# Cross-attention scores from one folded matrix per head, four heads in one matmul

## The chip, the cores and the metric

The kernel runs on one NeuronCore of a Trainium2 chip. Its time is the device time of one execution in microseconds. Times of a kernel are given as the median of several runs; a profiled execution has a time of its own, and its trace a span from the first to the last instruction.

## The reference, cut to what matters

The network has four blocks on 16 sequences of 128 tokens with 128 features; everything is f32. The change is in the second attention of the first block:

```python
def mha(xq, ctx, wq, wk, wv, wo, bo):              # H = 16 heads, DH = 64
    q = (xq @ wq).reshape(b, sq, H, DH).transpose(0, 2, 1, 3)
    k = (ctx @ wk).reshape(b, sk, H, DH).transpose(0, 2, 1, 3)
    v = (ctx @ wv).reshape(b, sk, H, DH).transpose(0, 2, 1, 3)
    scores = jnp.einsum('bhqd,bhkd->bhqk', q, k) / math.sqrt(DH)
    attn = jax.nn.softmax(scores, axis=-1)
    out = jnp.einsum('bhqk,bhkd->bhqd', attn, v)
    return out.transpose(0, 2, 1, 3).reshape(b, sq, INNER) @ wo + bo

h1 = adaln(x, t, norm1_w, norm1_b)
x = mha(h1, h1, ...attn1...) + x                   # self: 128 keys a sequence
h2 = adaln(x, t, norm2_w, norm2_b)
x = mha(h2, context, ...attn2...) + x              # cross: 77 keys a sequence
```

Since each score is h2 Wq_h (ctx Wk_h)^T for head h, it can also be computed as h2 (Wq_h Wk_h^T) ctx^T, with a 128 x 128 matrix per head. A gated feed-forward, a mixture of experts, slot attention and a second mixture of experts follow.

## The kernel before, in words

Attention works in 16 groups (`NG`), each of two sequences (`GB`): groups 0 to 7 are the self-attention of all 16 sequences, groups 8 to 15 the cross-attention. Here they are called the self half and the cross half. A unit is one sequence of one group; 32 units run one after the other.

`attn_prologue` (L235) makes what a group needs. It normalizes the tokens (za, on VectorE), transposes them (ta, L224) and applies scale and shift on ScalarE into hT (tile `ha`, L251), features on partitions. Then it projects on TensorE: queries with eight 128-column weight blocks against 256 tokens, keys with eight blocks against 256 (self) or 154 (cross) tokens, two blocks to a PSUM tile `pq` (L267), each tile read out by one ScalarE copy (L268); and values `pv` (L272, L276). A 128-column block holds two heads, on partitions 0 to 63 and 64 to 127 of `q` and `k`.

`scores` (L279) is called twice for a unit, for eight heads each (`hg`, here a head half). Eight matmuls with 64 contraction rows, alternating between the two halves of the partitions, write a PSUM tile `s` of two banks (L286). Softmax follows: VectorE's maximum (L294) and subtraction (L296), ScalarE's exp (L297), VectorE's sum and reciprocal (L299, L300), GpSimd's multiplication (L301). `attend_t` (L304) transposes the weights (te, L311), with one copy on ScalarE and one on VectorE (L312); `attend_v` (L315) multiplies by the values (po, L321), with a copy of the first head half on ScalarE and of the second on VectorE (L325); `attn_project` (L327) applies wo (ya, L331) and adds to `r`.

The loop at L379 runs one unit behind: the prologue of the next group is issued with the first unit of a group, the scores of the next unit come ahead of the transposes of this one, and the output projection is that of the unit before. The source order is not the final one: a scheduler places the instructions of each engine when the program is built, so pieces of scores lie between projections and po matmuls in the trace.

Pools that matter: PSUM `psS` (tag s, two tiles of two banks), `psT` (transposes, two), `psM` (tag mm, two: projections, values, po, ya); SBUF `zp` (tags z and h, two each), `att` (tags q, k, v, two each). The weights of both attentions are loaded at the start, four tiles of 128 x 2048 (`w_att`, L115, L121); `_layout` (L1061) arranges them on the host, wq beside wk for each attention.

Of the kernel before, what the change touches and what calls it, by code (L numbers as in the profile page):

```python
# [10 lines left out]
F32 = mybir.dt.float32  # L11
# [7 lines left out]
P = 128  # L19
B = 16  # L20
D = 128
NC = 77
H = 16
DH = 64
# [32 lines left out]
def pixart_kernel(  # L57
# [174 lines left out]
    GB = 2  # L232
    GT = GB * P

    def attn_prologue(g, ap_):  # L235
        ph, gi = divmod(g, B // GB)
        b0 = gi * GB
        rg = r[:, b0 : b0 + GB, :]
        z = zp.tile([P, 4, D], F32, name=f"za{g}", tag="z")
        if ph == 0:  # L240
            xg = x0[:, b0 : b0 + GB, :]
            rs, mean = ln_stats(xg, P, GB, f"i{g}")
            normalize(rg, xg, rs, mean, GB)
        rs, mean = ln_stats(rg, P, GB, f"j{g}")
        normalize(z, rg, rs, mean, GB)
        row_add(rg, R_BO1 if ph == 0 else R_BO2, GB)
        t = transpose_n(z, P, GB, f"a{g}")
        hT = zp.tile([P, 512], F32, name=f"ha{g}", tag="h")
        for i in range(GB):
            b = b0 + i  # L250
            S.activation(  # L251
                hT[:, i * P : (i + 1) * P], t[:, i, :], AF.Identity,
                bias=ada_sh[:, ph, b : b + 1], scale=ada_sc[:, ph, b : b + 1],
            )
        hT = hT[:, :GT]
        nk = P if ph == 0 else NC
        kvT = hT if ph == 0 else ctxT[:, b0 * NC : (b0 + GB) * NC]
        wqk, wvo = w_att[2 * ph], w_att[2 * ph + 1]
        qT = ap_.tile([P, 8, GT], F32, name=f"q{g}", tag="q")
        kT = ap_.tile([P, 8, GT], F32, name=f"k{g}", tag="k")  # L260
        v = ap_.tile([P, GB, H, DH], F32, name=f"v{g}", tag="v")
        for dst, src, w0, n in ((qT, hT, 0, GT), (kT, kvT, 1024, GB * nk)):
            for c in range(0, 8, 2):
                pq = psM.tile([P, 2, 256], F32, name=f"pq{g}_{w0}_{c}", tag="mm")
                for j in range(2):
                    w = w0 + (c + j) * P
                    PE.matmul(pq[:, j, :n], lhsT=wqk[:, w : w + P], rhs=src, start=True, stop=True)  # L267
                S.copy(dst[:, c : c + 2, :n], pq[:, :, :n])  # L268
        for i in range(GB):
            for hh in range(2):  # L270
                pv = psM.tile([P, 8, DH], F32, name=f"pv{g}_{i}_{hh}", tag="mm")
                PE.matmul(  # L272
                    pv[:nk].rearrange("p h d -> p (h d)"), lhsT=kvT[:, i * nk : (i + 1) * nk],
                    rhs=wvo[:, hh * 512 : (hh + 1) * 512], start=True, stop=True,
                )
                S.copy(v[:nk, i, hh * 8 : (hh + 1) * 8, :], pv[:nk])  # L276
        return dict(ph=ph, b0=b0, nk=nk, qT=qT, kT=kT, v=v, wo=wvo, g=g)

    def scores(st, i, hg, ap_):  # L279

        nk, nm = st["nk"], f"{st['g']}_{i}_{hg}"
        ps = psS.tile([P, 2, 512], F32, name=f"s{nm}", tag="s")
        for j in range(4):
            for par in range(2):
                h0, c = par * DH, 4 * hg + j
                PE.matmul(  # L286
                    ps[:, par, j * nk : (j + 1) * nk],
                    lhsT=st["qT"][h0 : h0 + DH, c, i * P : (i + 1) * P],
                    rhs=st["kT"][h0 : h0 + DH, c, i * nk : (i + 1) * nk],
                    start=True, stop=True,  # L290
                )
# [12 lines left out]
    def attend_t(st, i, hg, e, ap_):  # L304

        nk, nm = st["nk"], f"{st['g']}_{i}_{hg}"
        eT = ap_.tile([P, 2, 4, P], F32, name=f"eT{nm}", tag="eT", bufs=3)
        for par in range(2):
            t = psT.tile([P, 4, P], F32, name=f"te{nm}_{par}", tag="t")
            for j in range(4):  # L310
                PE.transpose(t[:nk, j, :], e[:, par, j, :], ident)  # L311
            (S.copy if par == 0 else V.tensor_copy)(eT[:nk, par], t[:nk])  # L312
        return eT
# [59 lines left out]
    if True:  # L373
        units = [(g, i) for g in range(NG) for i in range(GB)]
        states = {0: attn_prologue(0, ap_)}
        e_next = [scores(states[0], 0, hg, ap_) for hg in range(2)]
        late = None
        glu_h = {}
        for n, (g, i) in enumerate(units):  # L379
            if i == 0:  # L380
                if g + 1 < NG:
                    states[g + 1] = attn_prologue(g + 1, ap_)
                else:
                    glu_h[0] = glu_prologue(0)
            e = e_next
            if n + 1 < len(units):
                g1, i1 = units[n + 1]
                e_next = [scores(states[g1], i1, hg, ap_) for hg in range(2)]
            oT = ap_.tile([P, 8, P], F32, name=f"oT{g}_{i}", tag="oT")
            eT = [attend_t(states[g], i, hg, e[hg], ap_) for hg in range(2)]  # L390
            if late:
                attn_project(*late)
            for hg in range(2):
                attend_v(states[g], i, hg, eT[hg], oT)
            late = (states[g], i, oT)
        attn_project(*late)

# [663 lines left out]
def _layout(a):  # L1061
    import numpy as np

    cat = np.concatenate

    def chunks(w):
        return cat(np.split(w, w.shape[0] // P, axis=0), axis=1)

    def column(*vs):
        return cat([v.reshape(-1, P).T for v in vs], axis=1)  # L1070

    l0, l1 = "L0_xcond_", "L1_xcond_"
    cols = column(
        *[a[f"{l0}norm{k}_b"] for k in (1, 2, 3)], a[l0 + "ff_b1"],
        *[a[l1 + n] for n in ("lnkv_g", "lnkv_b", "lnq_g", "lnq_b", "lnm_g", "lnm_b", "bk", "bv", "bq", "b1")],
    )
    rows = cat(
        [a[l0 + n].ravel() for n in ("attn1_bo", "attn2_bo", "ff_b2")]
        + [a[l1 + n].ravel() for n in ("q_mu", "q_logsig", "lnp_g", "lnp_b", "bu", "b2")]
        + [a["cond_1024"].ravel(), a["L0_ffn_rb"], a["L1_ffn_b_gate"], np.arange(8, 0, -1, dtype=np.float32)]  # L1080
    )[None]
    attn = []
    for k in ("attn1_", "attn2_"):
        attn.append(cat([a[l0 + k + "wq"], a[l0 + k + "wk"]], axis=1))
        attn.append(cat([a[l0 + k + "wv"], chunks(a[l0 + k + "wo"])], axis=1))
    f = "L0_ffn_"
    gs = [a[f + "sg"], *a[f + "rg"]]
    us = [a[f + "su"], *a[f + "ru"]]
    ds = [a[f + "sd"], *a[f + "rd"]]

    def wide(w):
        return cat([w, np.zeros((w.shape[0], IP - I0), np.float32)], axis=1)

    moe0 = [cat([wide(g.T), wide(u.T), chunks(wide(d).T)], axis=1) for g, u, d in zip(gs, us, ds)]

    moe1 = [
        cat([w1, chunks(w2), b1.reshape(-1, P).T, np.broadcast_to(b2, (P, D))], axis=1)
        for w1, w2, b1, b2 in zip(*[a["L1_ffn_" + n] for n in ("W1", "W2", "b1", "b2")])
    ]
# [36 lines left out]
```

## Time and profile before

| | |
|---|---|
| median of 3 runs | 962.75 us (961.74 to 963.99) |
| profiled execution | 961.27 us, span 959.5 us |
| mean granted TensorE clock | 0.939 |
| attention ends at about | 488 us of the span |
| PE L267 (projections) | 97.3 us with 256 columns, 22.7 us with 154 columns busy |
| PE L286 (scores) | 45.5 us in the self half, 41.5 us in the cross half busy |
| ACT L268 copies | 584 ns (128 x 512), 412 ns (128 x 308) each |

PE is TensorE's matmuls, PEld its weight loads, DVE VectorE, ACT ScalarE, POOL GpSimd. Busy time on PE counts modelled ends that overlap the next start, so lengths are best read from start to start. In the group lines, "64*128" stands for the contraction rows and output columns of the array in use, "out<-in" for tiles by name. The chain is the work that ended last, followed back from the end.

### The profile page before, as it was taken

The numbers are of one execution on the slowest core, as the hardware profiler recorded it, in microseconds if no ns is written. First come the engines' busy times: TensorE is split into PE (matmuls) and PEld (weight loads), VectorE is DVE, ScalarE is ACT, GpSimd is POOL, SyncE is SP. The second block draws the span as 40 slices with busy tenths as digits, with TensorE's granted clock in tenths as the row PEclk, the third lists the DMA queues.
The fourth block names the chain that finished last, engine by engine and source line by source line (L and its number), as shares of the span: only waits on it lengthen the run. The fifth ranks groups of instructions, "written<-read, shape, count | busy, mean of one in ns | idle before, by whom it ended". The sixth has DMA issues, their size and how long they took to land.

```text
span 959.5 us, 16967 instructions
## 1 busy us (share of the span) xinstructions
PE 830.1 (87%) x6155; PEld 660.3 (69%) x6155; DVE 646.5 (67%) x1946; ACT 416.5 (43%) x873; POOL 369.9 (39%) x416
## 2 busy tenths in 40 slices
PE   5799999999999999999999978999746677775597
PEld 4477767677687777777866647999645556654586
DVE  4896668766775654555867794555687776768454
ACT  2445554455444444554342211444135767552132
POOL 2442323222322211233252206776254544443476
PEclk9899999999999999999999988999859998976699
DMA  8100000000000000000020015998300000012794
GB/s 325 40 2 1 1 1 2 1 1 1 1 2 1 1 1 2 1 1 1 2 71 12 23 61 166 320 331 271 99 1 1 1 1 1 1 31 58 253 341 149
DMA packets 29422, 61.87 MB, mean 64 GB/s; under 512 B 4250, under 2 KB 17901, under 8 KB 28699
## 3 DMA queue, kind: packets, MB, share of 16 engines
q1 hardware_dynamic: 25067, 51.70, 15.9%
q0 software_dynamic: 4272, 9.09, 3.1%
q8 instruction: 49, 0.80, 0.3%
q14 instruction: 34, 0.28, 0.1%
HBM read 54.01 MB, written 7.23 MB: 64 GB/s over the span
## 4 chain that ended last, share of the span: by engine, by line
PE 56%; DVE 21%; POOL 8%; DMA 7%; ACT 4%; issue 4%; SPq 0%; POOLq 0%; ACTq 0%; DVEq 0%
PE pq L267 11%; PE s L286 6%; PE po L321 5%; PE pv L272 5%; PE te L311 5%; PE ya L331 4%; DMA res<-ysm,tom 3%; PE gum L735 2%; PE h1n L979 2%; ACT eT L312 2%; DMA zsm<-tok,frmm 2%; PE su L898 2%; DMA zsn<-tok,frmn 2%; PE ynn L994 1%; POOL ym L170 1%
## 5 line engine op out<-in xcount | busy, mean ns | idle before, releaser
L301 POOL TENSOR_TENSOR e<-e,ri 128x1024 f32<-128x1024 f32 (+1 forms) x64 | 99.9, 1562 | 297.5 <-DVE ri L300 129.1
L294 DVE TENSOR_REDUCE mx<-s 128x8 f32<-128x1024 f32 (+1 forms) x64 | 64.3, 1006 | 95.7 <-PE s L286 95.7
L267 PE MATMUL pq<-ha,wa 128*128 128x256 f32 x384 | 97.3, 406 | 0.9 <-ACT ha L251 0.9
L286 PEld LDWEIGHTS s<-k,q 64*128 64x128 f32 x1024 | 69.9, 187 | 40.6 <-issue 40.5
L286 PE MATMUL s<-k,q 64*128 64x128 f32 (+1 forms) x1024 | 87.0, 287 | 8.1 <-DVE e L296 8.1
L311 PE MATMUL te<-ident,e 128*128 128x128 f32 (+1 forms) x512 | 75.7, 280 | 12.9 <-ACT eT L312 12.0
L267 PEld LDWEIGHTS pq<-ha,wa 128*128 128x128 f32 x384 | 70.6, 198 | 19.0 <-ACT q L268 3.6
L299 DVE TENSOR_REDUCE ri<-e 128x8 f32<-128x1024 f32 (+1 forms) x64 | 64.0, 1001 | 21.0 <-ACT e L297 20.8
L331 PE MATMUL ya<-wa,oT 128*128 128x128 f32 x512 | 72.4, 275 | 0.0
L311 PEld LDWEIGHTS te<-ident,e 128*128 128x128 f32 (+1 forms) x512 | 55.6, 144 | 23.7 <-ACT eT L312 8.5
L312 ACT COPY eT<-te 128x512 f32<-128x512 f32 (+1 forms) x64 | 37.3, 582 | 79.6 <-PE te L311 79.5
L321 PE MATMUL po<-eT,v 128*64 128x128 f32 (+1 forms) x1024 | 69.9, 278 | 0.0
L297 ACT ACTIVATE e<-e 128x1024 f32<-128x1024 f32 (+1 forms) x64 | 56.9, 891 | 29.5 <-DVE e L296 28.6
L296 DVE TENSOR_TENSOR e<-s,mx 128x1024 f32<-128x1024 f32 (+1 forms) x64 | 64.3, 1007 | 3.9 <-DVE mx L294 0.5
L331 PEld LDWEIGHTS ya<-wa,oT 128*128 128x128 f32 x512 | 64.4, 192 | 0.4 <-ACT oT L325 0.4
L321 PEld LDWEIGHTS po<-eT,v 128*64 128x64 f32 (+1 forms) x1024 | 56.4, 136 | 7.2 <-ACT oT L325 0.8
L735 PE MATMUL gum<-zTnm,wm 128*128 128x128 f32 x456 | 61.3, 275 | 0.0
L735 PEld LDWEIGHTS gum<-zTnm,wm 128*128 128x128 f32 x456 | 56.8, 192 | 0.3 <-ACT zTnm L650 0.2
L268 ACT COPY q<-pq 128x512 f32<-128x512 f32 x64 | 37.3, 584 | 45.3 <-PE pq L267 45.3
L636 POOL DMA_INDIRECT zsm<-tok,frmm x38 | 36.9, 970 | 34.1 <-DVE secm L614 21.1
L276 ACT COPY v<-pv 128x512 f32<-128x512 f32 (+1 forms) x64 | 37.4, 584 | 21.8 <-PE pv L272 21.1
L312 DVE COPY eT<-te 128x512 f32<-128x512 f32 (+1 forms) x64 | 42.7, 669 | 5.3 <-PE te L311 5.3
(368 smaller groups left out, 1805.6 us busy)
## 6 DMA issues: line engine op xcount, KB each, us to landing
wm<-in_moe_w_dram SPq DMA_DIRECT2D x38, 576.0 KB, 5.1
wn<-in_moe_w_dram SPq DMA_DIRECT2D x23, 578.0 KB, 5.5
wa<-in_attn_w_dram SPq DMA_DIRECT2D x4, 1024.0 KB, 7.5
ygm<-res SPq DMA_DIRECT2D x8, 256.0 KB, 3.8
tok<-stm SPq DMA_DIRECT2D x4, 258.0 KB, 3.3
tok<-stn SPq DMA_DIRECT2D x4, 258.0 KB, 3.2
x<-in_x_dram SPq DMA_DIRECT2D x8, 128.0 KB, 7.1
cb<-in_rows_dram SPq DMA_DIRECT2D x1, 1024.0 KB, 8.7
```

What stands on the lines that cost most here:

```text
L267: PE.matmul(pq[:, j, :n], lhsT=wqk[:, w : w + P], rhs=src, start=True, stop=True)
L286: PE.matmul(ps[:, par, j * nk : (j + 1) * nk], lhsT=st["qT"][h0 : h0 + DH, c, i * P : (i + 1) * P], rhs=st["kT"][h0 : h0 + DH, c, i * nk : ...
L294: V.tensor_reduce(mx, pv, AX.X, ALU.max)
L296: V.tensor_tensor(e, pv, mx.unsqueeze(3).to_broadcast([P, 2, 4, nk]), ALU.subtract)
L297: S.activation(e, e, AF.Exp, scale=1.0 / math.sqrt(DH))
L299: V.tensor_reduce(ri, e, AX.X, ALU.add)
L301: G.tensor_tensor(e, e, ri.unsqueeze(3).to_broadcast([P, 2, 4, nk]), ALU.mult)
L311: PE.transpose(t[:nk, j, :], e[:, par, j, :], ident)
L312: (S.copy if par == 0 else V.tensor_copy)(eT[:nk, par], t[:nk])
L321: PE.matmul(po[par * DH : (par + 1) * DH, j, :], lhsT=st["v"][:nk, i, 8 * hg + 2 * j + par, :], rhs=eT[:nk, par, j, :], start=True, stop=True,
L331: PE.matmul(y, lhsT=oT[:, c, :], rhs=st["wo"][:, 1024 + c * D : 1024 + (c + 1) * D], start=(c == 0), stop=(c == 7),)
L735: PE.matmul(ps[j][:, c * P : (c + 1) * P], lhsT=w[:, k : k + P], rhs=zT, start=True, stop=True)
```

## The change

For the cross half only, the weights of queries and keys are multiplied on the chip. `fold(w, hg)` runs twice, at units 8 and 9 (in the self half, group 4): eight matmuls with 64 contraction rows give one 128 x 128 matrix for each of eight heads, in a PSUM tile of tag s; one ScalarE and one VectorE copy of 128 x 512 write them over the loaded weights. For that, `_layout` stores wq and wk of the second attention transposed and interleaved; sizes and loads stay.

The prologue of a cross group then has no query projection: `qT` is hT itself. `kT` takes one 128-row block per head, sixteen matmuls of 154 columns, three to a PSUM tile, six ScalarE copies. A head half's scores are two matmuls with 128 contraction rows, four heads (4 x 77 = 308 columns) each, in place of eight with 64 rows. The loop's statements are written out, in the same order as before.

```diff
+        if ph == 0:
...
+        else:
+            qT = hT
+            kT = ap_.tile([P, H, GB * NC], F32, name=f"k{g}", tag="k")
+            for c in range(0, H, 3):
+                m = min(3, H - c)
+                pq = psM.tile([P, 3, GB * NC], F32, name=f"pk{g}_{c}", tag="mm")
+                for j in range(m):
+                    w = (c + j) * D
+                    PE.matmul(pq[:, j, :], lhsT=wqk[:, w : w + D], rhs=kvT, start=True, stop=True)
+                S.copy(kT[:, c : c + m, :], pq[:, :m, :])
...
+    def fold(w, hg):
+        ps = psS.tile([P, 2, 512], F32, name=f"fold{hg}", tag="s")
+        wp = w[:, hg * 1024 : (hg + 1) * 1024]
+        for j in range(4):
+            for par in range(2):
+                h0 = par * DH
+                PE.matmul(
+                    ps[:, par, j * D : (j + 1) * D],
+                    lhsT=wp[h0 : h0 + DH, (4 + j) * D : (5 + j) * D], rhs=wp[h0 : h0 + DH, j * D : (j + 1) * D],
+                    start=True, stop=True,
+                )
+        for par, copy in enumerate((S.copy, V.tensor_copy)):
+            copy(wp[:, par * 512 : (par + 1) * 512], ps[:, par, :])
...
     def scores(st, i, hg, ap_):
...
-        for j in range(4):
+        if st["ph"] == 1:
+            for par in range(2):
+                h0 = 8 * hg + 4 * par
+                PE.matmul(
+                    ps[:, par, : 4 * nk].rearrange("p (j k) -> p j k", k=nk),
+                    lhsT=st["qT"][:, i * P : (i + 1) * P],
+                    rhs=st["kT"][:, h0 : h0 + 4, i * nk : (i + 1) * nk],
+                    start=True, stop=True,
+                )
+        for j in range(4 if st["ph"] == 0 else 0):
...
         for n, (g, i) in enumerate(units):
+            if n in (8, 9):
+                fold(w_att[2], n - 8)
...
     for k in ("attn1_", "attn2_"):
-        attn.append(cat([a[l0 + k + "wq"], a[l0 + k + "wk"]], axis=1))
+        if k == "attn1_":
+            attn.append(cat([a[l0 + k + "wq"], a[l0 + k + "wk"]], axis=1))
+        else:
+            q, kk = (chunks(a[l0 + k + w].T) for w in ("wq", "wk"))
+            attn.append(cat([q[:, :512], kk[:, :512], q[:, 512:], kk[:, 512:]], axis=1))
```

More of the change, by code (lines that the diff above doesn't have):

```diff
@@ L258, in attn_prologue @@
         wqk, wvo = w_att[2 * ph], w_att[2 * ph + 1]
-        qT = ap_.tile([P, 8, GT], F32, name=f"q{g}", tag="q")
-        kT = ap_.tile([P, 8, GT], F32, name=f"k{g}", tag="k")
         v = ap_.tile([P, GB, H, DH], F32, name=f"v{g}", tag="v")
[L262 to L268, printed above, removed]
+        if ph == 0:
+            qT = ap_.tile([P, 8, GT], F32, name=f"q{g}", tag="q")
+            kT = ap_.tile([P, 8, GT], F32, name=f"k{g}", tag="k")
+            for dst, src, w0, n in ((qT, hT, 0, GT), (kT, kvT, 1024, GB * nk)):
+                for c in range(0, 8, 2):
+                    pq = psM.tile([P, 2, 256], F32, name=f"pq{g}_{w0}_{c}", tag="mm")
+                    for j in range(2):
+                        w = w0 + (c + j) * P
+                        PE.matmul(pq[:, j, :n], lhsT=wqk[:, w : w + P], rhs=src, start=True, stop=True)
+                    S.copy(dst[:, c : c + 2, :n], pq[:, :, :n])
+        else:
[8 more added lines that the diff above has]
+                S.copy(kT[:, c : c + m, :], pq[:, :m, :])
         for i in range(GB):
@@ L385, in pixart_kernel @@
             e = e_next
-            if n + 1 < len(units):
+            more = n + 1 < len(units)
+            if more:
                 g1, i1 = units[n + 1]
-                e_next = [scores(states[g1], i1, hg, ap_) for hg in range(2)]
+                e_next = [None, None]
             oT = ap_.tile([P, 8, P], F32, name=f"oT{g}_{i}", tag="oT")
-            eT = [attend_t(states[g], i, hg, e[hg], ap_) for hg in range(2)]
+            eT = [None, None]
+            if more:
+                e_next[0] = scores(states[g1], i1, 0, ap_)
+            if more:
+                e_next[1] = scores(states[g1], i1, 1, ap_)
+            eT[0] = attend_t(states[g], i, 0, e[0], ap_)
+            eT[1] = attend_t(states[g], i, 1, e[1], ap_)
             if late:
                 attn_project(*late)
-            for hg in range(2):
-                attend_v(states[g], i, hg, eT[hg], oT)
+            attend_v(states[g], i, 0, eT[0], oT)
+            attend_v(states[g], i, 1, eT[1], oT)
             late = (states[g], i, oT)
```

## The prediction

> **What bounds the kernel now.** I read the page first, then the busy time of each engine by stretch, then TensorE's timeline of one group of the cross half, then the matmul rows by shape. The page says how much of the chain that ended last is TensorE, and on which lines.
>
> ```profile
> PE 830.1 (87%) x6155; PEld 660.3 (69%) x6155; DVE 646.5 (67%) x1946; ACT 416.5 (43%) x873; POOL 369.9 (39%) x416
> ...
> PE 56%; DVE 21%; POOL 8%; DMA 7%; ACT 4%; issue 4%; SPq 0%; POOLq 0%; ACTq 0%; DVEq 0%
> PE pq L267 11%; PE s L286 6%; PE po L321 5%; PE pv L272 5%; PE te L311 5%; PE ya L331 4%; DMA res<-ysm,tom 3%; PE gum L735 2%; PE h1n L979 2%; ACT eT L312 2%; DMA zsm<-tok,frmm 2%; PE su L898 2%; DMA zsn<-tok,frmn 2%; PE ynn L994 1%; POOL ym L170 1%
> ```
>
> The projections (pq, L267) and the scores (s, L286), the two things that the change touches, lead the chain. By stretch, 266 to 471 us is the cross half; the row gives length, then busy time of PE, PEld, DVE, ACT, POOL, then the granted clock:
>
> ```profile
> 266.00:471.00 205.00, 201.81 (x1790) 160.15 (x1791) 122.58 (x250) 97.81 (x176) 51.53 (x45) 1.00 0.01 1
> 488.00:960.00 472.00, 373.02 (x2395) 306.29 (x2393) 317.80 (x1267) 189.33 (x488) 230.12 (x294) 0.88 0.34 111
> ```
>
> PE is busy in 201.8 of 205 us at full clock, DVE in 122.6, ACT in 97.8: the cross half is a stream of matmuls with little else in its way. The part after attention does not change. One group of the stream, TensorE alone (start, length, tile, count of records):
>
> ```profile
> 331.57 1.97 PE L321 MATMUL po<-eT,v 77*64 77x128 f32 x32
> 333.47 0.44 PE L224 MATMUL ta<-ident,za 128*128 128x128 f32 x2
> 333.84 1.11 PE L286 MATMUL s<-k,q 64*128 64x77 f32 x14
> 334.88 3.80 PE L267 MATMUL pq<-ha,wa 128*128 128x256 f32 x16
> 338.52 0.77 PE L267 MATMUL pq<-ctxT,wa 128*128 128x154 f32 x4
> 339.21 0.45 PE L286 MATMUL s<-k,q 64*128 64x77 f32 x4
> 339.59 2.09 PE L267 MATMUL pq<-ctxT,wa 128*128 128x154 f32 x12
> 341.51 1.02 PE L272 MATMUL pv<-wa,ctxT 128*77 128x512 f32 x2
> 342.47 0.45 PE L286 MATMUL s<-k,q 64*128 64x77 f32 x4
> 342.85 2.84 PE L272 MATMUL pv<-wa,ctxT 128*77 128x512 f32 x6
> 345.61 0.89 PE L286 MATMUL s<-k,q 64*128 64x77 f32 x10
> 346.43 1.10 PE L311 MATMUL te<-ident,e 128*77 128x128 f32 x8
> ...
> 350.53 1.09 PE L321 MATMUL po<-eT,v 77*64 77x128 f32 x16
> 351.56 0.44 PE L286 MATMUL s<-k,q 64*128 64x77 f32 x2
> 351.93 1.09 PE L321 MATMUL po<-eT,v 77*64 77x128 f32 x16
> 352.95 2.01 PE L286 MATMUL s<-k,q 64*128 64x77 f32 x30
> 354.89 1.10 PE L311 MATMUL te<-ident,e 128*77 128x128 f32 x8
> ```
>
> The next block of po with x32 starts at 358.93, so a group lasts 27.36 us. Lengths overlap by the modelled end, so I go from start to start. A matmul in f32 shows as two records (eight query matmuls, x16). Scores come in six visits, most of them two to seven matmuls put between projections by the build-time scheduler. Where I speak of the new order, it is that of the changed kernel's built queues.
>
> The cost of a record by width comes from its duration:
>
> ```profile
> L267 PE MATMUL pq<-ha,wa x384: 379/379/796, 13.3 to 447.8; 128*128 128x256 f32 x192
> L267 PE MATMUL pq<-ctxT,wa x128: 294/294/398, 256.3 to 450.8; 128*128 128x154 f32 x128
> ```
>
> With 592 ns for 512 columns (pv, L272) the slope is (592-294)/(512-154) = 0.832 ns a column, and 379 at 256 lies on the line. The ya blocks (eight records of 128 columns from 348.38 to 349.27) give 0.111 us, 4 ns over the slope. So a record that follows its like takes 0.832 x columns + 4 ns: 0.132 us at 154, 0.217 at 256, 0.430 at 512, and, estimated, 0.260 at 308.
>
> **What the Trainium skill says.** In the Trainium skill, "FP8 and Floating Point Precision", TensorE Precision Notes: a true f32 product takes four passes; the two records of 0.832 ns a column each agree with it. The Trainium skill, "TensorEngine Tiling (Array Packing)", Key Properties: tiles work side by side, and "Changing tiling mode (not just tile) drains the TensorE". The trace agrees with both: eight pairs of 64-row score matmuls take 1.94 us (352.95 to 354.89), 0.22 us a pair with some 0.15 over, while a lone one takes 0.37 (351.56) and a lone pair 0.38 (339.21). I take 0.22 a pair and 0.15 a visit, with 0.09 more for the first block after it. The Trainium skill, "PSUM — Partial Sum Buffer", Engine vs sequencer instructions: the queues of ScalarE, VectorE and GpSimd are strict FIFO. The trace agrees: an exp whose operand DVE had ready at 348.24 starts at 349.12, when the eT copy ahead of it is through. The waits below rest on it.
>
> **The change part by part, for a group of the cross half.**
>
> *Query projections, removed.* 334.88 to 338.52: 3.64 us. Their four ACT copies (584 ns each) go too; ACT had room. hT now lives until the scores; its pool has two buffers, and the earlier group's scores precede the next group's prologue but one, so no wait is added.
>
> *Key side, replaced.* Before: 0.69 + 1.92 = 2.61 us. After: sixteen matmuls of 154 columns are 32 x 0.132 = 4.22 us. They come in six chunks of up to three, each read out by one ACT copy of 462 columns, estimated at 0.54 us between the page's rows of 412 ns at 308 and 584 at 512. With two buffers, a chunk's buffer is free 0.29 (record's duration) + 0.04 + 0.54 + 0.04 = 0.91 us after its last record starts; TensorE wants it after 0.13 + 6 x 0.132 = 0.92. That is no margin, and the weight load (which the trace shows waiting 0.21 us on ACT in such places) is no longer pulled ahead. I put two losses of 0.12 a group: 4.47. Bounds: none (4.22) to five of 0.25 (5.5). Difference +1.86.
>
> *Scores.* Before: 1.04 + 0.38 + 0.38 + 0.82 + 0.37 + 1.94 = 4.93 us. After: per head half two matmuls with all 128 rows, four records of 308 columns: 4 x 0.260 = 1.04, four times a group 4.16. So -0.77. The pure work rises (four halves of 0.89 were 3.56); the fall is the visits' overhead. Unknown: the keys are read as four pieces of 77 with a stride of 154, which no matmul of this stretch does. Bounds: 0.260 a record, or twice that; below is excluded, as the columns must stream. I take 0.260, the keys being read at full rate inside each piece.
>
> *Mode changes around them.* pv: 0.96 + 2.76 = 3.72 becomes 8 x 0.430 + 0.1 = 3.54, -0.18. In the new order ta stands between the two po blocks: 1.03 + 0.37 + 1.02 = 2.42 for 1.90 + 0.37, +0.15. Scores between po's cost one change to po more, +0.09.
>
> Sum: -3.64 + 1.86 - 0.77 - 0.18 + 0.15 + 0.09 = -2.49 us. Seven groups have all of it: -17.4. The first prologue of the cross half stands among scores of the self half, which stay as they are: about -2.0. The last scores, outside any projection, and the first cost 4 x 0.52 = 2.08 for 1.94 each: +0.2. Together -19.2.
>
> *Who could be late next.* Softmax: the first half's scores now end only after the last key chunk, but before the values; then DVE max 0.80, subtract 0.80, ACT exp (behind two value copies) 0.73, DVE sum and reciprocal 1.0. DVE is through 4.3 us after those scores, and the second half's scores land after 3.5 (values) + 1.04 + 0.25 = 4.8. Slack 0.5 us. The transposes need that half 8 us later. Before, DVE took 346.54 to 351.37 for the second half, POOL 1.22, ready at 352.76 against 356.37 needed; the same 3.6 us remain.
>
> *The fold, added.* Two folds of eight 64-row matmuls, cut by the new order into 4, 1 and 3 among po's: 0.60 + 0.40 + 0.60 = 1.6 each. The first gathers that group's score visits (3.5 us in all with their mode changes, 2.2 after), so +0.35; the second cuts a po block in two, +1.97. Each has an ACT copy (584 ns) and a DVE copy (671 ns). Behind the second DVE copy wait the next scores, which need its buffer: about 0.6. In the first group, the scores' last piece moves behind the values, and DVE's max, subtract, max (1.22 each) stand ahead of its eT copy, which the transposes await: about 1.0. Sum +3.9, bounds 2 and 7. Both lie in the self half, where PE is also the bound.
>
> *Kept at nothing.* The stored weights have the same size and one DMA each. The keys' tile grows from 8,192 to 9,856 bytes a partition. What follows attention starts earlier by the gain.
>
> Total -19.2 + 3.9 = -15.3. The profiled execution took 961.27 (span 959.5): 946.0. It lies 1.48 below the median of 962.75, so I forecast 947.5.
>
> **Rivals.** *Gain given to waits.* The chunks' copies have no margin and DVE's slack is 0.5 us. If each of five chunks waits 0.25 and DVE adds 0.3 a group, the gain shrinks by 1.3 x 8 = 10: 958. For it: pq already waits 5.1 us in all for ACT's q copies and 3.2 for the k copies. Against: ACT is busy in under half of the stretch. *Slower: the strided read.* If TensorE reads the keys' four pieces at half rate, a score record takes 0.52 us: 16 x 0.26 = 4.2 us more a group, 33 us in eight: 981. It decides from 2.49 - 3.9/8 = 2.0 us a group, that is a record above 0.385 us. For it: the row is not in this trace. Against: pieces of 308 bytes are long. *Better than forecast.* No chunk waits and the folds cost only their matmuls: 947.5 - 2 - 2 = 943.
>
> **Chances.** Forecast 0.65 (944 to 952), waits 0.22 (952 to 961, most of it still over 0.2% faster; 0.2% is about what a measurement of this kernel tells from no change), better 0.06, strided read or a like price 0.07. Faster 0.90, same 0.03, slower 0.07. The range for 8 in 10 runs from 942 to 956: it takes in the bounds of the folds and the better half of the waits.
>
> **What would show it.** In the profile after: no 128x256 pq in the cross half; a group of 24.9 us from po to po; 308-column score records with a duration near 0.832 x 308 + 166 = 422 ns, in step 0.26; key blocks 4.5 us a group with ACT waits of some 0.1; PE above 97% busy there. Wrong if the score records stand apart by more than 0.26, if the transposes wait for e on POOL or DVE, or if the groups of the folds last over 5 us longer.

## The result and the profile after

| | before | changed |
|---|---|---|
| median | 962.25 us (961.7 to 963.99) | 945.89 us (945.44 to 947.1) |
| profiled execution, its span | 961.27, 959.5 us | 947.1, 945.4 us |
| mean granted TensorE clock | 0.939 | 0.937 |
| first transpose of weights (te) | 50.95 us | 51.41 us |
| group of units 8 and 9 (the folds) | 30.83 us | 34.59 us |
| group of the cross half | 27.36 us | 25.02 us |
| last block of ya, the end of attention | 487.85 us | 475.37 us |
| from there to the end | 471.6 us | 470.0 us |

The ratio of the times is 0.9829, 95% interval 0.9812 to 0.9846. A group's length is the distance of two po blocks two units apart in TensorE's timeline. The experiments below ran on several chips. On one of them (all times above 980 us) the part after attention takes some 508 to 513 us in every trace, and the kernel before has a median of 1003 to 1005 us there. So a time is compared only with the kernel before on the same chip, and lengths inside attention are compared throughout.

From the page of the changed kernel, the chain that ended last:

```profile
PE 57%; DVE 21%; POOL 7%; DMA 7%; ACT 4%; issue 4%; SPq 1%; POOLq 0%; ACTq 0%; DVEq 0%
PE po L360 6%; PE pq L268 5%; PE pv L284 5%; PE te L350 4%; PE ya L370 4%; PE pk L279 4%; PE s L316 4%; PE gum L783 4%; PE s L325 2%; PE h1n L1027 2%; PE ynm L794 2%; ACT eT L351 2%; DMA zsn<-tok,frmn 2%; PE glu L479 2%; DMA zsm<-tok,frmm 2
```

The projections were 11% of the chain (pq, all of both halves); now they are 5% in the self half (pq) and 4% for the keys of the cross half (pk). TensorE is 57% of the chain as it was 56%: the same engine sets the time, with 352 records less (5803 for 6155). The stretch of the cross half, with the columns of the prediction's table (length, busy time of PE, PEld, DVE, ACT, POOL, then the granted clock):

```profile
266.00:455.00 189.00, 185.85 (x1424) 144.60 (x1422) 123.77 (x251) 89.26 (x163) 51.92 (x45) 1.00 0.00 1
```

The seven full groups of the cross half are 7 x 2.34 = 16.4 us shorter, and just as full: 185.85 of 189 us is 98%. What follows attention has the same records (2394 for 2395) and the same busy time on PE (373.6 us for 373.0). One group, TensorE alone, to set against the one in the prediction:

```profile
320.71 1.09 PE L360 MATMUL po<-eT,v 77*64 77x128 f32 x16
321.73 0.79 PE L316 MATMUL s<-k,ha 128*128 128x308 f32 x2
322.45 1.09 PE L360 MATMUL po<-eT,v 77*64 77x128 f32 x16
323.48 1.84 PE L316 MATMUL s<-k,ha 128*128 128x308 f32 x6
325.15 1.03 PE L350 MATMUL te<-ident,e 128*77 128x128 f32 x8
...
331.61 1.05 PE L279 MATMUL pk<-ctxT,wa 128*128 128x154 f32 x6
332.50 0.69 PE L316 MATMUL s<-k,ha 128*128 128x308 f32 x2
333.02 3.79 PE L279 MATMUL pk<-ctxT,wa 128*128 128x154 f32 x26
336.65 0.69 PE L316 MATMUL s<-k,ha 128*128 128x308 f32 x2
337.18 3.63 PE L284 MATMUL pv<-wa,ctxT 128*77 128x512 f32 x8
340.65 1.21 PE L316 MATMUL s<-k,ha 128*128 128x308 f32 x4
341.70 1.03 PE L350 MATMUL te<-ident,e 128*77 128x128 f32 x8
...
345.73 0.44 PE L360 MATMUL po<-eT,v 77*64 77x128 f32 x4
```

No 128x256 projection is left. The keys take 331.61 to 332.50 and 333.02 to 336.65, 0.89 + 3.63 = 4.52 us. The scores are five visits: 0.72 + 1.67 + 0.52 + 0.53 + 1.05 = 4.49 us. The duration of a score matmul, from the line's own view (least, median, most in ns):

```profile
L316 PE MATMUL s<-k,ha x128: 422/423/531, 272.1 to 458.8; 128*128 128x308 f32 x128
```

It is the 422 ns that a row of 308 columns without gaps would have had; four records in a row take 1.05 us, 0.262 each. The keys read as four pieces of 77 cost nothing over that. The copies that empty the key chunks:

```profile
L280 ACT COPY k<-pk x48: 293/544/547, 256.6 to 437.0; 128x462 f32<-128x462 f32 x40, 128x154 f32<-128x154 f32 x8
...
who waited for it (us, times):
  PEld pv L284: 1.7, 7
  PEld pk L279: 0.2, 1
```

544 ns for 462 columns; the weight loads waited for them 1.9 us in the whole run. In each group the trace has two key records, each behind the first of a new chunk, that start 0.235 us apart where others start 0.131 apart; with the records ahead of them they lose 0.23 us together, which is the forecast's two losses of 0.12. So the chunks nearly keep up, with no room. The other 0.10 of the 4.52 us is lost at the entry from po (six records take 0.89 us for 0.79). VectorE at the second head half's maximum, in the same group:

```profile
341.89 0.80 DVE L333 TENSOR_REDUCE mx<-s 128x8 f32<-128x616 f32 x1 [0.53 <-PE s L316]
```

VectorE waits 0.53 us for TensorE there, and not the other way round.

### The profile page after: what moved, and what is told of

Read it like the earlier page. It is cut to its first block, busy times and chain, and to the rows that moved or that the text cites. A ratio compares the mean times of both kernels' runs of the same rounds, so it can differ in the third digit from the quotient of the medians.

```text
span 945.4 us, 16234 instructions
## 1 busy us (share of the span) xinstructions
PE 816.6 (86%) x5803; PEld 645.2 (68%) x5803; DVE 646.9 (68%) x1948; ACT 407.2 (43%) x859; POOL 369.2 (39%) x416
## 4 chain that ended last, share of the span: by engine, by line
PE 57%; DVE 21%; POOL 7%; DMA 7%; ACT 4%; issue 4%; SPq 1%; POOLq 0%; ACTq 0%; DVEq 0%
PE po L360 6%; PE pq L268 5%; PE pv L284 5%; PE te L350 4%; PE ya L370 4%; PE pk L279 4%; PE s L316 4%; PE gum L783 4%; PE s L325 2%; PE h1n L1027 2%; PE ynm L794 2%; ACT eT L351 2%; DMA zsn<-tok,frmn 2%; PE glu L479 2%; DMA zsm<-tok,frmm 2%
## 5 line engine op out<-in xcount | busy, mean ns | idle before, releaser
L333 DVE TENSOR_REDUCE mx<-s 128x8 f32<-128x1024 f32 (+1 forms) x64 | 64.3, 1005 | 78.7 <-PE s L325 39.8
L360 PE MATMUL po<-eT,v 128*64 128x128 f32 (+1 forms) x1024 | 72.7, 279 | 0.1
L268 PE MATMUL pq<-ha,wa 128*128 128x256 f32 x256 | 65.6, 410 | 1.0 <-ACT ha L251 0.9
L268 PEld LDWEIGHTS pq<-ha,wa 128*128 128x128 f32 x256 | 47.7, 201 | 13.8 <-ACT q L269 2.3
L325 PE MATMUL s<-k,q 64*128 64x128 f32 x512 | 44.1, 291 | 9.5 <-DVE e L335 8.9
L325 PEld LDWEIGHTS s<-k,q 64*128 64x128 f32 x512 | 34.5, 188 | 24.3 <-issue 23.5
L705 POOL DMA_INDIRECT res<-ysm,tom x38 | 37.3, 981 | 15.9 <-ACT ysm L798 7.7
```

Source lines behind the costliest of these rows:

```text
L325: PE.matmul(ps[:, par, j * nk : (j + 1) * nk], lhsT=st["qT"][h0 : h0 + DH, c, i * P : (i + 1) * P], rhs=st["kT"][h0 : h0 + DH, c, i * nk : ...
L360: PE.matmul(po[par * DH : (par + 1) * DH, j, :], lhsT=st["v"][:nk, i, 8 * hg + 2 * j + par, :], rhs=eT[:nk, par, j, :], start=True, stop=True,
```

## The experiments

All are edits of the changed kernel. "a0_changed" is the changed kernel once more (945.61 us, ratio 0.984, 0.981 to 0.987; attention ends at 475.1 us; groups 25.02, 30.83 and, with the folds, 34.6 us), so two traces of one kernel differ by 0.3 us at attention's end, and by 2.8 us in the part after it (470.0 and 467.2). In some traces the granted clock also falls to half for a few microseconds at about 55 us of the span (see the last experiment), which moves attention's end by up to some 3 us. The lengths of groups given below lie behind that place.

**The folds left out.**

```diff
-            if n in (8, 9):
-                fold(w_att[2], n - 8)
```

> The changed kernel (945.9 us) without the two folds: the weights of queries and keys are left unmultiplied, so the cross scores are those of other matrices; all else is the same. Theory: the self half is bound by TensorE, the folds cost some 3.7 us there (3.9 in the prediction), so 942.2. Rival: the fold lies in waits that the self half has anyway, so 945.4 or more.

Measured: 984.7 us, ratio 0.9811 (0.9786 to 0.9836). The group of units 8 and 9 falls to 30.83 us, 3.76 less, and attention ends at 471.1 us. So the folds cost 3.76 us, all of it in that group: 1.09 in the first of its two units and 2.67 in the second.

**The query projections made again, and not used.**

```diff
             qT = hT
+            qx = ap_.tile([P, 8, GT], F32, name=f"q{g}", tag="q")
+            for c in range(0, 8, 2):
+                ...
+                    PE.matmul(pq[:, j, :], lhsT=wqk[:, w : w + P], rhs=hT, start=True, stop=True)
+                S.copy(qx[:, c : c + 2, :], pq)
```

> The changed kernel with the query projections of the cross half put back (eight matmuls and four ScalarE copies for a group), computed and used by nothing. Theory: the cross half is a stream of matmuls without cover, so the whole 3.64 us a group come back, 29 us in eight groups: 975, above the kernel before (962). Rival: the gain was that waits between engines went, and a projection lies partly in them: under 962.

Measured: 1018.23 us, ratio 1.0127 (1.0089 to 1.0164), slower than the kernel before. Attention ends at 504.5, 29.1 us later. That this is the expected 29 is chance: 3.0 us of it are lost by the second unit (its po starts at 68.01 us for 65.03), where the clock fell in this trace. A group lasts 28.32 us, 3.30 more. In TensorE's timeline of a group:

```profile
346.39 2.94 PE L278 MATMUL px<-ha,wa 128*128 128x256 f32 x12
349.17 0.69 PE L323 MATMUL s<-k,ha 128*128 128x308 f32 x2
349.69 1.02 PE L278 MATMUL px<-ha,wa 128*128 128x256 f32 x4
350.55 4.74 PE L286 MATMUL pk<-ctxT,wa 128*128 128x154 f32 x32
```

The projections take 2.78 + 0.86 = 3.64 us, to 0.01 what they took before. The other 0.34 is given back elsewhere in the reordered group, whose scores lie in fewer places. Since work of 3.64 us makes the group 3.30 longer, nothing else was about to be late there: TensorE's own sum is the length of a group. With the queries kept, one matrix per head would lose: the whole gain is their absence.

**One head at a time, with all 128 rows.**

```diff
-                PE.matmul(ps[:, par, : 4 * nk]..., rhs=st["kT"][:, h0 : h0 + 4, i * nk : (i + 1) * nk], ...)
+                for j in range(4):
+                    PE.matmul(ps[:, par, j * nk : (j + 1) * nk], ..., rhs=st["kT"][:, 8 * hg + 4 * par + j, i * nk : (i + 1) * nk], ...)
```

> The changed kernel with the scores of one head in each matmul (eight of 77 columns, 128 rows) in place of four heads in one (two of 308). Theory: a record of few columns costs no less than 0.111 us, the step seen at 128 columns[...]: sixteen records are 1.78 us a head half for 1.04, less 0.35 a group for scores that now stay together: 2.6 us a group, 967. Rival: only columns count, 0.832 x 77 + 4 = 68 ns a record, 1.09 us a head half: 944 to 948.

Measured: 1003.79 us, ratio 1.0013 (0.9988 to 1.0039): the gain is gone. Attention ends 16.1 us later, 1.4 of it lost by the second unit; a group takes 27.05 us, 2.03 more.

```profile
327.69 3.80 PE L316 MATMUL s<-k,ha 128*128 128x77 f32 x32
331.32 1.04 PE L350 MATMUL te<-ident,e 128*77 128x128 f32 x8
```

32 records take 3.63 us, 0.113 each, though 77 columns at 0.832 ns and 4 ns would be 0.068. The blocks of te and ya, at 128 columns, have steps of 0.11 too: at 77 a record is no cheaper than at 128. With all 128 rows in use, that floor falls on each head alone, so "four heads at once" is not an ornament of the change; it carries it. The scores alone rose by 2.63, to 7.12 us a group. The group's rise stayed under the expected 2.6 because these scores lie in three places for five, so that the po blocks aren't split (3.79 us for 4.10), and the rest of the order gave back some 0.3.

**64 of the 128 rows, four heads at once.**

```diff
+                d0 = par * DH
-                    lhsT=st["qT"][:, ...], rhs=st["kT"][:, h0 : h0 + 4, ...],
+                    lhsT=st["qT"][d0 : d0 + DH, ...], rhs=st["kT"][d0 : d0 + DH, h0 : h0 + 4, ...],
```

> The changed kernel with scores that use 64 of the 128 contraction rows (rows 0 to 63 for the first four heads, 64 to 127 for the others), so half of each sum is left out; order and columns are as they were. Theory: matmuls of a pair run side by side, which takes 1.05 us off a group, while three visits among full matmuls pay for a change of mode, 0.24 us each, and one more 0.15: together -0.2 us a group, 944.5. Rival: a change of mode costs nothing, -1.05 a group, 937.5.

Measured: 988.3 us, ratio 0.9849 (0.9824 to 0.9875); attention ends at 474.9, as in a0_changed, but a group takes 25.22 us, 0.20 more: the first units and the last ones, outside the full groups, came out shorter by some 1.3. The timeline of a group holds both halves of the answer:

```profile
331.76 0.79 PE L317 MATMUL s<-k,ha 64*128 64x308 f32 x2
332.48 3.90 PE L279 MATMUL pk<-ctxT,wa 128*128 128x154 f32 x26
336.31 0.79 PE L317 MATMUL s<-k,ha 64*128 64x308 f32 x2
337.03 3.69 PE L284 MATMUL pv<-wa,ctxT 128*77 128x512 f32 x8
340.65 0.80 PE L317 MATMUL s<-k,ha 64*128 64x308 f32 x4
341.38 1.10 PE L351 MATMUL te<-ident,e 128*77 128x128 f32 x8
```

Two matmuls in opposite halves run beside each other: four records take 0.73 us in place of 1.05. A lone one takes 0.72 in place of 0.52, and the blocks after it are longer too (pv 3.62 for 3.47, the 26 key records 3.83 for 3.63). The pairs' saving is paid out again for changes of the tiles in use, an estimated 1.25 us a group, the difference between +0.20 and the rival's -1.05. So part of what the changed kernel gains in its scores is that they have the tile shape of their neighbours. The first expectation had the sign wrong: it took too little for the changes.

**The folds before the loop.**

```diff
-        ps = psS.tile([P, 2, 512], F32, name=f"fold{hg}", tag="s")
+        ps = [psM.tile([P, 512], F32, name=f"fold{hg}_{par}", tag="mm") for par in range(2)]
...
+        for hg in range(2):
+            fold(w_att[2], hg)
         for n, (g, i) in enumerate(units):
-            if n in (8, 9):
-                fold(w_att[2], n - 8)
```

> The changed kernel with both folds ahead of the loop, in four one-bank PSUM tiles of the projections' pool with all four copies on ScalarE, where the trace shows TensorE idle for 7 us (28 to 35 us of the span). Theory: the fold costs 3.76 us only because TensorE is the bound at units 8 and 9; early it lies in the idle time, attention ends near 471.5 and the time falls by 3 to 4 us. Rival: the start is a chain of softmax and projections, and ScalarE's four copies (2.3 us) stand in it: no gain.

Measured: 945.03 us, ratio 0.9815 (0.9785 to 0.9844); attention ends at 475.1 as in a0_changed. The group of units 8 and 9 is down to 30.83 us, but the first te comes at 54.52 us in place of 51.16, and the first full group takes 30.95 for 28.98. The cost moved and stayed. In the timeline the first of the two folds lies in TensorE's early wait for softmax (now 5.12 us for 7.33), but the second stands behind that wait, in 2.3 us among the next scores, and the projections behind it start at 41.23 us for 35.99. How much of the later te is the fold and how much the new order was not separated.

**Every second key chunk read by VectorE.**

```diff
-                S.copy(kT[:, c : c + m, :], pq[:, :m, :])
+                (S.copy if c % 2 == 0 else V.tensor_copy)(kT[:, c : c + m, :], pq[:, :m, :])
```

> The changed kernel with every second copy of the cross half's key tiles on VectorE in place of ScalarE. Theory: the key blocks (4.52 us a group for 4.22 of pure streaming) lose little to the copies, so 0.2 us a group and under 2 us in all can be had; VectorE's slack of 0.5 us ahead of the second head half's maximum is used up in part. Rival: the copies set the pace of the key blocks; then 0.5 us a group or more, 4 us in all.

Measured: 948.44 us, ratio 0.9868 (0.9835 to 0.9901); a group takes 25.22 us, 0.20 more; attention ends at 476.7. Both expectations had it faster. The rows of VectorE's copies and of the key matmuls' idle time:

```profile
L280 DVE COPY k<-pk x24: 319/640/640, 258.2 to 438.3; 128x462 f32<-128x462 f32 x16, 128x154 f32<-128x154 f32 x8
...
  PEld pk L279: 2.8, 16
```

A VectorE copy takes 640 ns, 96 more than ScalarE's, and weight loads now wait 2.8 us, 16 times, where they waited 0.2, once. VectorE was idle ahead of nearly all of these copies, so they did not queue. The two losses of a group grew from 0.23 to 0.43 us together, which is the 0.20. It is the time from a chunk's last matmul to its free buffer that counts, with 0.91 against 0.92 us in the prediction; a second reader doesn't shorten that, and a slower one lengthens it.

**Two heads to a chunk.**

```diff
-            for c in range(0, H, 3):
-                m = min(3, H - c)
-                pq = psM.tile([P, 3, GB * NC], F32, name=f"pk{g}_{c}", tag="mm")
+            for c in range(0, H, 2):
+                m = min(2, H - c)
+                pq = psM.tile([P, 2, GB * NC], F32, name=f"pk{g}_{c}", tag="mm")
```

> The changed kernel with two heads a key tile in place of three (eight tiles of 308 columns, eight copies of 412 ns for six). Theory: four records take 0.524 us, but a tile's buffer is free 0.29 + 0.04 + 0.41 + 0.04 = 0.78 us after its last record starts, wanted after 0.655; each second tile waits 0.25, so a cross group goes from 25.0 to 25.7 us and attention ends 5 to 6 us later. Rival: the copies are hidden behind the scores put between the key tiles: 25.0.

Measured: 994.39 us, ratio 0.9884 (0.9848 to 0.992); a group takes 25.48 us, 0.46 more, and attention ends at 479.3. Of the 4.2 us to a0_changed, 0.6 are lost by the second unit. In TensorE's timeline the 32 key records take 0.62 + 4.41 = 5.03 us for 4.52, and the weight loads wait 4.7 us for the copies, 22 times. Three times a group two records in a row start late, by 0.25 us together, as the first expectation had it: 0.75. The changed kernel loses 0.23 in the same way, so 0.52 of it is new, and 0.46 show in the group. The copies of the three-head chunk are at the edge and these are past it.

**The same change in the self half too**, with the first attention's folds before the first prologue (its weights stored as the second's).

```diff
-        if st["ph"] == 1:
+        if True:
...
+        for hg in range(2):
+            fold(w_att[0], hg)
         states = {0: attn_prologue(0, ap_)}
```

> The same change made to the self half as well: its weights are folded ahead of the first prologue, its keys take one 128-row block per head against 256 tokens, its scores are two matmuls of 512 columns a head half. Theory: the gain comes from columns, not from the form: with as many keys as tokens the projections cost the same (32 records of 0.217 us, 6.9, for 7.2), while the scores stream 16 x 0.430 = 6.9 us a group for 5.4 with their mode changes. A self group goes from 30.8 to 32 us, and with the fold at the start attention ends 10 to 14 us later. Rival: the gain comes from fewer mode changes and instructions, which the self half has as well: a self group under 30.8.

Measured: 943.83 us, ratio 0.9819 (0.9791 to 0.9847); attention ends at 473.8, 1.3 us earlier than in a0_changed. Self groups take 30.25 to 30.84 us, the one with the folds 34.12; the largest single gain is where the self half passes into the cross half (25.83 us for 27.22). Neither expectation gives that. With 128 keys, the scores must get longer, and did. TensorE before, in a unit of the self half:

```profile
207.33 1.97 PE L321 MATMUL po<-eT,v 128*64 128x128 f32 x32
209.23 2.06 PE L286 MATMUL s<-k,q 64*128 64x128 f32 x32
211.22 1.09 PE L311 MATMUL te<-ident,e 128*128 128x128 f32 x8
...
215.88 0.66 PE L311 MATMUL te<-ident,e 128*128 128x128 f32 x4 [1.44 <-ACT eT L312]
```

and the same unit with the change in both halves:

```profile
211.44 1.97 PE L350 MATMUL po<-eT,v 128*64 128x128 f32 x32
213.34 3.70 PE L306 MATMUL s<-k,ha 128*128 128x512 f32 x8
216.87 1.04 PE L340 MATMUL te<-ident,e 128*128 128x128 f32 x8
...
219.98 0.66 PE L340 MATMUL te<-ident,e 128*128 128x128 f32 x4
```

The scores take 3.53 us for 1.99, and yet from po to the last transposes the unit takes 8.54 for 8.55 (and to the next po 9.57 for 9.58): the wait of 1.44 us ahead of the last transposes is gone, and the longer scores stand in its place. The name beside the wait is ScalarE's copy of the first transposes' results (eT). TensorE, ScalarE and VectorE before, around the same wait one group earlier:

```profile
183.46 1.06 ACT L297 ACTIVATE e<-e 128x1024 f32<-128x1024 f32 x1 [1.75 <-DVE e L296]
184.42 0.57 ACT L312 COPY eT<-te 128x512 f32<-128x512 f32 x1
184.47 0.68 DVE L312 COPY eT<-te 128x512 f32<-128x512 f32 x1
185.04 0.66 PE L311 MATMUL te<-ident,e 128*128 128x128 f32 x4 [1.45 <-ACT eT L312]
```

TensorE goes on 0.05 us after ScalarE's copy ends, at 184.99; VectorE's copy ends only at 185.15, so it is not what TensorE waited for. ScalarE's copy stands in its queue behind the exp of the next scores, and that exp waited 1.75 us for VectorE's subtraction. So a self group holds some 1.45 us in which TensorE waits for ScalarE's queue, and longer scores fit into it. The prediction's remark that TensorE bounds the self half too holds for all of a group but this.

**The fold in four pieces, placed ahead of that wait** (units 3, 5, 7 and 9, into a tile of its own).

```diff
             eT[0] = attend_t(states[g], i, 0, e[0], ap_)
+            if n in (3, 5, 7, 9):
+                fold_piece(w_att[2], (n - 3) // 2)
             eT[1] = attend_t(states[g], i, 1, e[1], ap_)
```

> The changed kernel with the fold cut into four pieces (four matmuls, one PSUM tile of the projections' pool, one ScalarE copy into a tile of its own), one in each of units 3, 5, 7 and 9, between the transposes of the first and the second head half. There TensorE waits 1.45 us in each self group for an eT copy that stands behind maximum, subtraction and maximum in VectorE's queue. Theory: a piece costs TensorE 0.89 and a change of mode 0.24, which that wait covers, so attention ends near 472 where the changed kernel has 475.1, and the time falls by 3 us. Rival: the waits are not spare, whatever is put there delays the copies after it: 475 or more.

Measured: 993.5 us, ratio 0.9894 (0.9856 to 0.9933); attention ends at 479.2, 4 us later than in a0_changed, not earlier.

```profile
157.25 0.61 PE L367 MATMUL ya<-wa,oT 128*128 128x128 f32 x4
159.48 0.66 PE L347 MATMUL te<-ident,e 128*128 128x128 f32 x4 [1.62 <-DVE eT L348]
159.97 1.50 PE L367 MATMUL ya<-wa,oT 128*128 128x128 f32 x12
```

The expectation put the wait down to VectorE's queue; in the kernel before and in the changed one it is ScalarE's copy, behind its exp, as shown above. In this kernel's order ScalarE's copy comes later, and it is VectorE's that TensorE waits for. The wait ends about when it did, 4.83 us after the unit's first te (4.67 before), and is 1.62 us long. The build-time order answered the piece by moving eight ya records from ahead of the wait to behind it (4 ahead and 12 behind, for 12 and 4 before): the fold took the place of other cover, and the wait stayed. One group of this kernel is 35.25 us: in the changed order it has a new wait of 1.88 us ahead of its projections, with a granted clock of 0.78 and 0.79 in the next stretches (132 to 136 and 136 to 140 us), and sixteen records of 256 columns take 5.34 us for 3.73. These 1.6 us, and 0.7 lost by the second unit at half clock, are no price of the pieces as such; without them attention would still end later than in a0_changed.

**Both.** The change in both halves, with the pieces of the second fold as in the last one.

```diff
+            fold(w_att[0], hg)
...
+                fold_piece(w_att[2], (n - 3) // 2)
```

> The kernel with the change in both halves, and the fold of the cross half in the same four pieces at the same places. Theory: in that kernel the longer scores of the self half have already taken up TensorE's wait (1.5 us of it), so the pieces are not covered: about 1.1 us each, 4.5 in all, against 3.3 for its fold at units 8 and 9, and attention ends at 475 where it was 473.8. Rival: the wait is there again, the pieces cost nothing: 470.5.

Measured: 990.52 us, ratio 0.9851 (0.9811 to 0.9891); attention ends at 476.1, 2.3 us later than with the change in both halves alone. The groups with pieces take 31.7 to 32.3 us. The wait was used up already, and the pieces are plain work there.

**Both folds of the second attention made first**, the fold's weights loaded ahead of the first attention's.

```diff
+    wa2 = load_w(attn_w[2], 2048, "wa2")
...
+        for hg in range(2):
+            fold(w_att[2], hg)
         states = {0: attn_prologue(0, ap_)}
...
-            if n in (8, 9):
-                fold(w_att[2], n - 8)
```

> The folds of wa2 and wa1 are both made ahead of everything else of the attention, in the idle time that TensorE has at the start of the changed kernel while the first tokens arrive; wa2 is loaded ahead of wa0 for that. Theory: the fold of wa2 then costs nothing where it stands now (the group of units 8 and 9 falls from 34.6 to 30.8 us), the first transposes and projections start within 0.5 us of where they start in the changed kernel, and attention ends at about 472 us against 475.1: about 942.5 us, ratio 0.980. Rival: the loads that are put later by it (wa0 behind wa2) hold the first projections by some 3 us, and attention ends at 475 as before: ratio 0.984.

Measured: 942.9 us, ratio 0.9795 (0.9754 to 0.9836); attention ends at 473.6, 1.5 us before a0_changed: between the two expectations. The group of units 8 and 9 takes 30.82 us, so the whole 3.76 are gone there, and the first projections start at 14.43 us in place of 13.45, 1.0 later. The rest of the loss comes at the first units. In TensorE's timeline:

```profile
53.93 0.77 PE L326 MATMUL s<-k,q 64*128 64x128 f32 x2 [3.49 <-DVE e L336]
```

The first te (49.35 us) is even 2.1 us earlier than in the changed kernel, but then TensorE waits 3.49 us for VectorE, where it waited 2.15 in the changed kernel. The stretch after it of this kernel (the granted clock is the third number from the end), and then of the changed one:

```profile
54.00:60.00 6.00, 6.00 (x36) 4.43 (x36) 4.57 (x6) 1.47 (x2) 1.90 (x1) 0.53 0.01 3
```

```profile
54.00:60.00 6.00, 5.32 (x52) 4.04 (x52) 6.00 (x8) 3.19 (x4) 1.25 (x1) 1.00 0.02 4
```

After the longer wait the clock is 0.53, and four transposes take 1.04 us where they took 0.59. The same records that took 54.65 to 58.24, 3.59 us, in the changed kernel take 53.93 to 60.04, 6.11: 2.5 us lost to the clock. The Trainium skill, "TensorE: Matmul & The Clock Gate", What's actually happening, says that the clock falls to half after an idle window of about 3.4 us. The traces do not bear out that the length of this wait decides. In the kernel with the queries projected again, TensorE waits 2.15 us at this place, as in the changed kernel, and the clock falls all the same:

```profile
54.79 0.77 PE L332 MATMUL s<-k,q 64*128 64x128 f32 x2 [2.15 <-DVE e L342]
```

```profile
56.00:60.00 4.00, 4.00 (x23) 2.78 (x23) 3.27 (x5) 0.59 (x1) 1.12 (x1) 0.50 0.00 0
```

There the same records take 54.79 to 61.26, 6.47 us. With one head at a time, in pieces of the fold and with two heads to a chunk, waits of 1.92, 2.15 and 2.22 us at this place were followed by a clock of 0.68, 0.61 and 0.63 between 56 and 60 us. So the 2.5 us are not shown to be a price of the fold's new place; what sets the fall is open.

This kernel has the lowest median of all, but its interval overlaps those of the changed kernel's two runs (0.9829 and 0.984): that it beats the change is not settled, only that attention ends 1.5 us earlier in its profile.

## Why the prediction was right

Forecast 947.5 us, measured 945.89. From profile to profile, -14.2 us against -15.3; from median to median, -16.4. The mechanism held: query projections gone, keys dearer, scores cheaper, on a TensorE that stayed 98% busy. That the median lies only 1.6 us from the forecast is in part luck. At attention's end the gain is 12.5 us for the 15.3 forecast, and the part after it, forecast to stay as long, was shorter by 1.6 in this trace and by 4.4 in that of a0_changed. Lengths in us, measured in the trace of the changed kernel:

| step | forecast | measured |
|---|---|---|
| group of the cross half | 24.87 | 25.02 |
| key side | 4.47 | 4.52 |
| ACT copy of 462 columns | 0.54 | 0.544 |
| scores of a group | 4.16 | 4.49 |
| score record: duration, step | 0.422, 0.260 | 0.423, 0.262 |
| values | 3.54 | 3.47 |
| VectorE's slack at the second maximum | 0.5 | 0.53 |
| folds | +3.9 | +3.76 |
| first prologue of the cross half | -2.0 | -1.87 |
| seven groups | -17.4 | -16.4 |
| last section | +0.2 | +1.6 |

*The scores were too cheap by 0.33 a group*, the one term that was mis-sized in the group. The forecast counted sixteen records of 0.260 and 0.09 for the change back to po. In the trace, two records between po blocks take 0.72 us, 0.20 over, and six after a po block 1.67, 0.10 over. A visit of scores to po's, with another tile shape, costs on entering as well as on leaving; the half-rows experiment prices the same effect from the other side. Half of it was made up for: by 0.07 in the values, 0.07 in te and ya, and the 0.09 for the change back to po, which did not come on top (that po block takes 1.03 us, for 1.02 before). A record's step of 0.262 us is, to the letter, over the 0.26 that the forecast named as a sign of being wrong; it is the forecast's rate to 1%, and far from the 0.385 at which the gain would go. The other two signs stayed away. TensorE's waits ahead of transposes are the same 0.16 us for ScalarE's copy as before (in five groups their weight load is held for GpSimd's e by 0.32, and TensorE stops no longer for it), and the group of the folds is 3.76 us longer, not 5.

*The last section* got 1.4 us longer not through scores but because the build-time order put a second matmul of the feed-forward (glu) into it, which also splits a po block (464.17 to 466.64, for 477.94 to 479.00 before). So the forecast's statement that what follows only starts earlier was not exact. Whether the moved work came back after attention, 1.6 us shorter here, can't be told: two traces of the changed kernel differ by 2.8 us there. At attention's end the table's steps make -12.9 with the first te 0.46 later: -12.5.

*The folds' sum was right, one of its waits was not.* The fold's eight matmuls in three pieces cost 1.80 and 1.63 us for 1.6 each. The wait behind the VectorE copy is 0.51 for 0.6. The wait of about 1.0 that the first fold's unit was to have ahead of its transposes is 0.17 in the trace:

```profile
177.01 0.66 PE L350 MATMUL te<-ident,e 128*128 128x128 f32 x4 [0.17 <-ACT eT L351]
...
189.25 0.65 PE L350 MATMUL te<-ident,e 128*128 128x128 f32 x4 [1.22 <-ACT eT L351]
```

The first unit still took 1.09 more, for 1.35 forecast: its pieces were dearer by 0.2, and gathering its scores saved 0.8 (3.19 to 2.39 us in TensorE's timeline) where the forecast had 1.3. So errors offset each other there, and the sum is right in part by luck. A second unit with no fold has the 1.45 us wait of the self half anyway, and with the second fold it is 1.22; the forecast had not seen that wait, and so took TensorE for the bound of the self half in full. It also named VectorE's copy as what the transposes would await; the 1.22 and 1.45 us are waits for ScalarE's.

*The rivals.* Waits of the chunks: they are there at 0.23 us a group, as forecast, and not with the rival's 1.3 more; VectorE was not late. The two chunk experiments show that the margin is as small as the prediction said (0.46 us a group with smaller chunks, 0.20 with a slower reader) and that it holds. The strided read is refuted by the record's step of 0.262 us. That step, and not the length of the pieces, is the evidence: the prediction's "pieces of 308 bytes are long" rested on no measurement. Nor do two records of 0.832 ns a column show by themselves that a product takes four passes; no sum rests on it. The better case, 943, needed cheap folds, and they were not.

## What to carry to other kernels

Where TensorE is 98% busy, a change of its work can be summed up record by record from start to start, and it comes out to 0.6% of a group (25.02 for 24.87), which is 6% of the change (2.34 for 2.49); what such a sum misses is the price of going from one tile shape to another and back, so count visits, not only records. Here a fold of two weight matrices paid because it removed a projection and because its wider scores stayed above the width at which a record stops getting cheaper (four heads of 77, not one). Before filling a wait of TensorE with work, look at what the build-time order will move out of it, and at which engine's instruction ends just ahead of the restart.

## What was not expected of the hardware

Four pieces of 77 columns with a stride of 154 are read at full rate by TensorE: 0.262 us a record, for an estimated 0.260 without gaps. An f32 record of 77 columns takes 0.113 us, no less than one of 128 (0.111). Two 64-row matmuls of 308 columns in opposite halves run beside each other (four records in 0.73 us for 1.05), and a lone one between 128-row blocks is dearer than one with 128 rows (0.72 us for 0.52, the changes of tile shape included). After a wait of 2.15 us at one place of the program the granted clock was 1.00 in the changed kernel's trace and 0.50 in another's (56 to 60 us).
